# A build-order planner with other costs and a wider urgent class, in an adaLN, Mamba and expert-mixture kernel

## The chip, the cores and the metric

The kernel runs on one core of a Trainium2 chip. A core has five engines, each with its own queue of instructions, which it works off strictly in order: TensorE (PE, matrix products and transposes), VectorE (DVE), ScalarE (ACT), GpSimd (POOL) and SyncE (SP, which here only issues transfers). An instruction whose inputs are not ready holds up everything behind it in its queue. The metric is the device time of one launch in microseconds. Times given as a median are of several unprofiled runs; durations of single instructions come from one profiled execution.

## What is computed

The input x has 4 sequences of 1024 tokens and 512 channels, all in float32. Cut to what matters:

```
mod = silu(c) @ wmod                        # six shifts, scales and gates per sequence
h = layernorm(x) * (1 + ca) + sa
u = causal depthwise convolution of h, 4 taps
dt, B, C = split(u @ xproj.T)               # 128 + 16 + 16
delta = softplus(dt @ dtproj.T + bias)
for every channel d and state n (16 of them), along the 1024 tokens:
    s[t] = exp(delta[t] * A[d, n]) * s[t-1] + delta[t] * B[t, n] * u[t]
y[t] = sum over n of s[t] * C[t, n]  +  u[t] * D_skip
x = x + ga * y
h = layernorm(x) * (1 + cb) + sb
logits = tanh(h @ Wg1.T) @ Wg2.T            # 8 experts, the best 2 per token, softmax of those two
out = sum over the two of score * (silu(h @ Wup[e].T + bup[e]) @ Wdown[e].T + bdown[e])
x = x + gb * out
```

## The kernel before

**Blocks and stages.** The tokens are cut into nine blocks (`BLOCKS`): two of 512 for each of the first three sequences, and 512, 384 and 128 for the last. They are numbered 0 to 8. Each block goes through four stages:

- `front(blk)`: layernorm, convolution, projection, delta. It ends with delta, delta times u (turned) and B in SBUF, and with C's 16 rows written to a scratch array in DRAM.
- The recurrence. It is cut into units, one for each block, channel group of 128 and state, 64 per block and 576 in all, numbered u. A unit is worked on by seven generators: `loads_c` (SP reads one row of C, spread over 128 partitions, tile `cq`, one for two units), `products_b` (ScalarE or GpSimd, tile `dB`), `decays` (ScalarE, the exponential, tile `h`), `inputs` (TensorE turns `dB` into PSUM, tile `pb`), `recurrences` (VectorE, a scan along the tokens), `products_c` (GpSimd, h times C, tile `hc`), `sums` (TensorE adds the `hc` of 16 states into PSUM, tile `acc`). The rings between them are short: 2 `pb`, 3 `hc`, and 4 each of `dB`, `cq` and `h`, of which the last three hold two units.
- `back(blk)` for blocks 0 to 7: VectorE adds the result to x (`residual`), layernorm, transposes (`second_norm`, `turned`), the router with its top two (`router`), each token's place in its expert's rows, and the scatter of the rows to DRAM by GpSimd's indirect transfers (tile `xs`). Beside it `spread` adds the biases and stores the sum (`x1d`).
- The experts. Blocks (0, 1), (2, 3), 4, 5, 6 and 7 form six groups, `GROUPS`, numbered 0 to 5. `tiles(g)` has SP load, for each tile of 128 rows, the rows and 1025 KB of one expert's weights (tile `w`, four buffers, a fifth after the last front), `expert` multiplies (tiles `px`, `pe`, `po`) and stores, and `combine` gathers each token's two rows (tile `xc`, GpSimd) and writes the output. Block 8 takes no tiles: `dense` runs all 8 experts over its 128 tokens (tiles `we`, `pue`, `poe`).

**What sets the order.** All of these are generators that yield a step (engine, cost, what must be there) before they issue its instructions. A planner, the class `Order`, runs while the kernel is built: it keeps a clock for each engine, reckons when each waiting step could begin, takes the engine that can begin first at time t0, and among the steps of that engine that could begin shortly after t0 picks the one with the earliest due time. The instructions are then laid down in that order, for good. The reckoned length of a step is its cost from formulas such as `t_scan` and `t_act`; if it is over 0.03 us, it is multiplied by `PACE` and `WAIT` is added (10% for TensorE, 0.06 us for VectorE, ScalarE and GpSimd). `HANDOFF` is added before another engine may use the result. Where a step can run on one of two engines (`products_b`, `either`, `both`), the planner also picks the engine by these numbers.

"Shortly" is 0.15 us (`TOGETHER`) for an ordinary step. A step whose due time is below `URGENT` (-1000) may begin up to 0.8 us later (`AHEAD`) and is still laid down first. `LAST` makes steps urgent: it is -20000 for the last two blocks, and is added to the due times of the residual, of the way through `back` with its router, of the transposes in `turned` and of the scatters. Tiles and combines have due times from a table, `TILES_DUE`, and do not use `LAST`.

The lines of the profile that matter: 950 scan, 967 product with C, 935 input transposes, 1006 sums, 868 load of C's row, 1040 residual, 1118 and 1253 two steps of the router that wait for other engines, 1335 scatter, 1380 and 1382 loads of a tile's rows and weights, 1448 second product of an expert, 1497 gather of a combine.

Of the kernel before, what the change touches and what calls it, by code (L numbers as in the profile page):

```python
# [30 lines left out]
NBLK = len(BLOCKS)  # L31
# [66 lines left out]

PE, DVE, ACT, POOL, SP = range(5)
HANDOFF = (0.30, 0.17, 0.22, 0.12, 0.0)  # L100
PACE = (1.1, 1.0, 1.0, 1.0, 1.0)
WAIT = (0.0, 0.06, 0.06, 0.06, 0.0)
TOGETHER = 0.15
URGENT = -1e3
AHEAD = 0.8
# [78 lines left out]
class Order:  # L184
# [34 lines left out]
    def run(self):  # L219
        while self.threads:  # L220
            can = [(b, th) for th in self.threads if (b := self.begins(th)) is not None]
            if not can:
                raise RuntimeError("no thread can go on: " + str([th[0].__name__ for th in self.threads]))
            t0, eng, _ = min(can, key=lambda c: c[0][0])[0]
            (t, _, cost), th = min(
                (
                    c
                    for c in can
                    if c[0][1] == eng and c[0][0] <= t0 + (AHEAD if c[1][3] < URGENT else TOGETHER)
                ),  # L230
                key=lambda c: c[1][3],
            )
            self.eng, kb = eng, th[1][4]
            if cost > 0.03:
                cost = cost * PACE[eng] + WAIT[eng]
            self.start = t
            self.free[eng] = t + cost
            self.fin = t + cost + HANDOFF[eng]
            if kb:
                self.moved[eng] = max(self.moved[eng], t + cost) + kb / KB_PER_US  # L240
                self.fin = max(self.moved[eng], t + cost + kb / KB_ALONE) + TRANSFER
            th[2] = self.fin
            th[3] += th[4]
            self.advance(th)
# [28 lines left out]
    return DUE[k] + (f - k) * 150.0 if k >= NBLK else DUE[k] + (f - k) * (DUE[k + 1] - DUE[k])  # L273


LAST = [-2e4 if blk >= NBLK - 2 else 0.0 for blk in range(NBLK)]


@with_exitstack
def adaln_mamba_moe_kernel(  # L280
# [32 lines left out]
    def event(*key):  # L313
        if key not in ev:
            ev[key] = Event()
        return ev[key]
# [542 lines left out]
    def due(u):  # L859
        return DUE[u // PER] + (u % PER + 1) * (DUE[u // PER + 1] - DUE[u // PER]) / PER  # L860
# [120 lines left out]
    def sums():  # L981

        for u in range(N_U):
# [31 lines left out]
            if n == NS - 1:  # L1015
                event("acc", blk, dc).t = o.fin
                o.spawn(residual(blk, dc), due(u) + LAST[blk])

# [17 lines left out]
    def residual(blk, dc):  # L1036
        n = BLOCKS[blk][2]
        yield step(DVE, t_dve(n), event("acc", blk, dc), event("xr", blk, dc // 2))
        xs = xr[blk][dc // 2].t[:, : n // P, dc % 2 * P : (dc % 2 + 1) * P]
        nc.vector.tensor_tensor(xs, xs, acc.pop((blk, dc))[:, :n].rearrange("p (t c) -> p t c", c=P), ALU.add)  # L1040
        acc_ring[dc % 2].give(2 * blk + dc // 2, o.fin)
        event("x1", blk, dc).t = o.fin
        x1_left[blk] -= 1
        if x1_left[blk] == 0:
            if blk + 1 < NBLK:
                o.spawn(back(blk), DUE[blk + 1] + LAST[blk], 1.2)
            else:
                o.spawn(dense(blk), DUE[blk + 1] + LAST[blk], 1.0)

# [110 lines left out]
    def second_norm(blk):  # L1160
# [9 lines left out]
        def turn(dc):  # L1170
            yield from turned(xn, n, dc, b, 3, 4, h2T.t[:, dc, :n], f"b{blk}")
            h2_in[dc].t = o.fin

        for dc in range(DC):
            o.spawn(turn(dc), DUE[blk + 1] + 8.0 + 2.0 * dc + LAST[blk], 2.0)
        return h2T, h2_in

    def back(blk):
# [136 lines left out]
        def scatter(t):  # L1315
            yield step(PE, t_tr(DC), banks, ring("t512B", 4).many(2), combined[g - N_XS])
            h2 = [t512("B", f"h2_{blk}_{t}_{k}") for k in range(2)]
            ph, tag = new_bank(f"ph_{blk}_{t}")
            for dc in range(DC):
                nc.tensor.transpose(ph[:, dc * P : (dc + 1) * P], h2T[:, dc, t * P : (t + 1) * P], ident)  # L1320
            turned_in = Event()
            turned_in.t = o.fin
            yield step(ACT, t_act(512))
            nc.scalar.copy(h2[0].t[:, :D], ph)
            copied = Event()
            copied.t = o.fin
            yield step(DVE, t_dve(512) + 0.15, after=[turned_in])
            nc.vector.tensor_copy(h2[1].t[:, :D], ph)
            for k in range(2):
                nc.vector.tensor_copy(h2[k].t[:, D:], sv[:, k, t : t + 1])  # L1330
            banks.give(tag, o.fin)
            for k in range(2):
                yield step(POOL, 1.2, copied, kb=256)
                nc.gpsimd.tensor_copy(idx[:, k, t : t + 1], to[:, k, t : t + 1])  # L1334
                i = nc.gpsimd.indirect_dma_start(  # L1335
                    out=xs_d[g],
                    out_offset=bass.IndirectOffsetOnAxis(ap=idx[:, k, t : t + 1], axis=0),
                    in_=h2[k].t,
                    in_offset=None,
                )  # L1340
                apart(f"token{g}", i)
                h2[k].done()
            left[0] -= 1
            if left[0] == 0:
                hb.done()
                scattered[g][0] -= 1
                if scattered[g][0] == 0:
                    event("rows", g).t = o.fin

        for t in range(nt):  # L1350
            o.spawn(scatter(t), DUE[blk + 1] + 28.0 + 3.0 * t + LAST[blk], 2.0)

# [378 lines left out]
```

## Time and profile before

| | |
|---|---|
| median of 3 runs | 1471.55 us (1467.81 to 1481.65) |
| the profiled execution | 1473.26 us, span 1471.5 us |
| granted TensorE clock, mean | 0.925 |
| start of the scans of blocks 0 to 8 | 67.7, 191.2, 331.3, 485.3, 646.6, 812.8, 979.1, 1144.1, 1285.7 us |
| last scan | 1387.6 us |
| last expert tile's second product | 1430.3 us |
| bytes moved | 321.65 MB, 219 GB/s over the span |

In the profile a name such as `hc<-h,cq` is a tile and what it is made from, a number such as L967 a line of the kernel, and "x576" a count. A row of waits names who waited, for whom, the sum in us, how often and the longest. A row of stretches gives the length, then for each engine the busy time and the count of its instructions, then TensorE's granted clock, the share of time in which the transfer engines were busy, and GB/s.

### The profile page before, as it was taken

To read this page: it belongs to the slowest core of one execution; us is meant where nothing else is said; L and a number is where in the kernel's file an instruction comes from. 1 tells how busy PE (TensorE), PEld (TensorE's weight loads), DVE (VectorE), ACT (ScalarE), POOL (GpSimd) and SP (SyncE) were. 2 spreads that over 40 slices of the span, in tenths; PEclk is the share of its full clock that TensorE was granted. 3 is DMA by queue.
4 is the path that set the end of the run, shared out by engine and by line. 5 is a ranking of instruction groups with operands and counts; after the bars stand their busy time and mean duration, and the time that the engine had idled before them with its cause. 6 is when DMAs were issued, how large, how long until landed. Compare 5 with 4: busy or idle time off the path is not lost. (4 is left out here: it accounts for less than half of the span.)

```text
span 1471.5 us, 24433 instructions
## 1 busy us (share of the span) xinstructions
PE 1236.6 (84%) x7716; PEld 931.7 (63%) x7716; DVE 1146.8 (78%) x1860; ACT 1041.7 (71%) x2086; POOL 1052.8 (72%) x1239
## 2 busy tenths in 40 slices
PE   5588777878788988988888888998798898888886
PEld 1447564656477766775667766786587776764653
DVE  3569999889887898998887888897879879556343
ACT  3679898689687684899676776888678877455210
POOL 1368897898687676888888656798788878656222
PEclk8699899889799998999699999999999999998798
DMA  4367664758688997654679968688999986986997
GB/s 175 101 161 157 136 160 101 197 127 199 140 243 283 292 273 202 213 159 101 197 257 313 309 210 204 219 269 246 262 252 271 281 221 219 337 249 200 298 311 200
DMA packets 141935, 321.65 MB, mean 219 GB/s; under 512 B 14899, under 2 KB 43475, under 8 KB 128998
## 3 DMA queue, kind: packets, MB, share of 16 engines
q1 hardware_dynamic: 111344, 254.35, 57.9%
q0 software_dynamic: 13888, 32.58, 9.9%
q10 hardware_dynamic: 16566, 33.08, 8.8%
q8 instruction: 63, 1.03, 0.3%
q14 instruction: 74, 0.61, 0.1%
HBM read 245.95 MB, written 82.40 MB: 223 GB/s over the span
## 5 line engine op out<-in xcount | busy, mean ns | idle before, releaser
L967 POOL TENSOR_TENSOR hc<-h,cq 128x512 f32<-128x512 f32 (+2 forms) x576 | 689.5, 1255 | 190.1 <-PE acc L1006 53.4
L920 ACT ACTIVATE h<-delta,a_neg 128x512 f32<-128x512 f32 (+2 forms) x576 | 370.8, 667 | 88.8 <-POOL state L975 44.9
L892 ACT ACTIVATE dB<-duT,bT 128x256 f32<-128x256 f32 x801 | 359.9, 499 | 77.2 <-PE pb L935 74.8
L935 PE MATMUL pb<-ident,dB 128*128 128x128 f32 x2048 | 344.6, 291 | 80.4 <-DVE h L950 64.3
L1006 PE MATMUL acc<-ident,hc 128*128 128x128 f32 x2048 | 340.9, 291 | 75.1 <-POOL hc L967 73.2
L950 DVE TENSOR_TENSOR_SCAN h<-h,state,pb 128x512 f32<-128x512 f32 (+2 forms) x320 | 330.6, 1054 | 50.9 <-PE pb L935 25.8
L935 PEld LDWEIGHTS pb<-ident,dB 128*128 128x128 f32 x2048 | 251.2, 149 | 169.3 <-DVE h L950 85.9
L1006 PEld LDWEIGHTS acc<-ident,hc 128*128 128x128 f32 x2048 | 250.5, 148 | 155.9 <-POOL hc L967 122.3
L950 DVE TENSOR_TENSOR_SCAN h<-h,pb 128x512 f32<-128x512 f32 x256 | 304.4, 1207 | 45.9 <-PE pb L935 37.2
L1420 PE MATMUL pe<-xT,w 128*128 128x128 f32 x1376 | 188.0, 282 | 6.5 <-ACT xT L351 4.8
L1420 PEld LDWEIGHTS pe<-xT,w 128*128 128x128 f32 x1376 | 174.1, 197 | 27.4 <-issue 14.2
L1448 PE MATMUL po<-w,hid 128*128 128x512 f32 x344 | 180.8, 612 | 6.6 <-DVE hid L1440 6.5
L899 POOL TENSOR_TENSOR dB<-duT,bT 128x512 f32<-128x512 f32 (+1 forms) x115 | 119.6, 1061 | 18.4 <-PE pb L935 12.4
L1497 POOL DMA_INDIRECT xc<-xs,idx x56 | 90.4, 1614 | 51.7 <-DMA xc<-xs,idx 29.8
L1458 DVE SCALAR_TENSOR_TENSOR xs<-po,xs,gbh 128x512 f32<-128x512 f32 x86 | 63.6, 740 | 39.7 <-PE po L1448 38.1
L1335 POOL DMA_INDIRECT xs<-h,idx x62 | 64.0, 1032 | 41.3 <-POOL idx L1334 9.2
L1448 PEld LDWEIGHTS po<-w,hid 128*128 128x128 f32 x344 | 54.1, 195 | 24.0 <-issue 11.3
L1438 ACT ACTIVATE th<-pe 128x256 f32<-128x256 f32 x86 | 32.2, 377 | 49.4 <-DVE pe L1431 49.2
L351 ACT COPY xT<-px 128x512 f32<-128x512 f32 x79 | 45.5, 577 | 25.0 <-PE px L1407 24.5
L975 POOL COPY state<-h 128x2 f32<-128x2 f32 x160 | 54.6, 341 | 0.1
L720 PE MATMUL pxd<-xpg,u 128*128 128x160 f32 x256 | 46.2, 329 | 9.4 <-issue 5.6
L1407 PE MATMUL px<-ident,xs 128*128 128x128 f32 x344 | 53.8, 284 | 0.3 <-DVE u L688 0.3
(196 smaller groups left out, 1533.5 us busy)
## 6 DMA issues: line engine op xcount, KB each, us to landing
w<-w_all SPq DMA_DIRECT2D x86, 1025.0 KB, 8.5
cq<-scr SPq DMA_DIRECT2D x224, 256.0 KB, 5.3
xs<-xs SPq DMA_DIRECT2D x86, 256.5 KB, 5.3
xs<-xs SPq DMA_DIRECT2D x86, 256.0 KB, 8.0
xs<-xc ACTq DMA_DIRECT2D x16, 1026.0 KB, 11.7
we<-w_all SPq DMA_DIRECT2D x8, 1025.0 KB, 12.3
xf<-in_x SPq DMA_DIRECT2D x32, 256.0 KB, 6.9
xr<-in_x SPq DMA_DIRECT2D x14, 512.0 KB, 8.9
```

Source lines behind the costliest of these rows:

```text
L892: nc.scalar.activation(dB[u // 2].t[:, t, :], duT_sb[blk][half].t[:, t, :], AF.Identity, scale=bT_sb[blk].t[:, t, n : n + 1],)
L899: engine().tensor_tensor(dB[u // 2].t[:, t0:t1, :], duT_sb[blk][half].t[:, t0:t1, :], bT_sb[blk].t[:, t0:t1, n].unsqueeze(2).to_broadcast( ...
L920: nc.scalar.activation(hs[u // 2].t[:, i, :ln], delta_sb[blk][half].t[:, i, :ln], AF.Exp, scale=a_neg[:, dc, n : n + 1])
L935: nc.tensor.transpose(pbs[u][:, t * P : (t + 1) * P], dB[u // 2].t[:, t, i * P : (i + 1) * P], ident)
L950: nc.vector.tensor_tensor_scan(h, h, pbs.pop(u)[:, :ln], 0.0 if t0 == 0 else state[:, n, dc : dc + 1], ALU.mult, ALU.add,)
L967: nc.gpsimd.tensor_tensor(hcs[u].t[:, :ln], hs[u // 2].t[:, i, :ln], cq[u // 2].t[:, :ln], ALU.mult)
L1006: nc.tensor.matmul(acc[blk, dc][:, t * P : (t + 1) * P], lhsT=src.t[:, t * P : (t + 1) * P], rhs=ident, is_transpose=True, start=False, st ...
L1335: i = nc.gpsimd.indirect_dma_start(out=xs_d[g], out_offset=bass.IndirectOffsetOnAxis(ap=idx[:, k, t : t + 1], axis=0), in_=h2[k].t, in_off ...
L1420: nc.tensor.matmul(pu[:, hc * P : (hc + 1) * P], lhsT=up[:, kc, hc * P : (hc + 1) * P], rhs=xT.t[:, kc, :], start=(kc == 0), stop=(kc == D ...
L1448: nc.tensor.matmul(po, lhsT=hid.t[:, hc * P : (hc + 1) * P], rhs=w.t[:, W_DN + hc * D : W_DN + (hc + 1) * D], start=(hc == 0), stop=(hc == ...
L1458: nc.vector.scalar_tensor_tensor(xs.t[:, :D], po, xs.t[:, D:], gbh[b].t, ALU.mult, ALU.mult)
L1497: nc.gpsimd.indirect_dma_start(out=a, out_offset=None, in_=xs_d[g], in_offset=bass.IndirectOffsetOnAxis(ap=idx_sb[blk][:, choice, t : t + ...
```

## The change

Two things. The planner's two corrections of a step's cost, `PACE` and `WAIT`, go, so that TensorE is reckoned at its full clock and the other engines without the 0.06 us. And `LAST` covers the last four blocks (5, 6, 7 and 8) in place of the last two (7 and 8). No operation, no buffer and no transfer is added or removed; the instructions are laid down in another order, and some steps fall to another engine. All later line numbers shrink by 4.

```
-PACE = (1.1, 1.0, 1.0, 1.0, 1.0)
-WAIT = (0.0, 0.06, 0.06, 0.06, 0.0)
...
             self.eng, kb = eng, th[1][4]
-            if cost > 0.03:
-                cost = cost * PACE[eng] + WAIT[eng]
             self.start = t
             self.free[eng] = t + cost
             self.fin = t + cost + HANDOFF[eng]
...
-LAST = [-2e4 if blk >= NBLK - 2 else 0.0 for blk in range(NBLK)]
+LAST = [-2e4 if blk >= NBLK - 4 else 0.0 for blk in range(NBLK)]
```

## The prediction

> **What bounds the kernel now.** I read the page's busy shares first, then its chain, then a table of stretches, one for each block of the recurrence (cut where the scans at multiples of 64 units start), because the shares are an average over unlike stages.
>
> ```profile
> PE 1236.6 (84%) x7716; PEld 931.7 (63%) x7716; DVE 1146.8 (78%) x1860; ACT 1041.7 (71%) x2086; POOL 1052.8 (72%) x1239
> ...
> PE 7%; DMA 5%; DVE 3%; issue 3%; POOL 2%; ACT 1%; SPq 0%; POOLq 0%; DVEq 0%; ACTq 0%
> ```
>
> Four engines are 71 to 84% busy, and the chain gives no engine more than 7%: no single engine sets the time. What sets it is how well five in-order queues fit together, and that is the thing the change redraws.
>
> ```profile
> core 0: us, PE busy (x) PEld busy (x) DVE busy (x) ACT busy (x) POOL busy (x), PEclk, DMA share, GB/s
> ...
> 812.80:979.10 166.30, 151.94 (x1014) 118.62 (x1013) 143.99 (x222) 126.10 (x245) 120.49 (x121) 0.97 0.79 235
> 979.10:1144.10 165.00, 147.27 (x979) 116.41 (x979) 135.25 (x215) 129.65 (x266) 136.09 (x156) 0.96 0.94 261
> 1144.10:1285.70 141.60, 126.93 (x828) 96.82 (x826) 110.54 (x211) 101.21 (x231) 106.14 (x149) 0.98 0.88 265
> 1285.70:1338.90 53.20, 47.16 (x275) 33.19 (x274) 34.23 (x106) 27.95 (x70) 31.88 (x61) 0.94 0.79 225
> 1338.90:1387.60 48.70, 40.52 (x171) 26.50 (x170) 21.04 (x53) 19.16 (x50) 20.77 (x38) 0.72 0.90 278
> 1387.60:1430.00 42.40, 35.59 (x205) 24.45 (x204) 16.98 (x46) 8.98 (x23) 11.09 (x18) 1.00 1.00 304
> ```
>
> Blocks 5, 6 and 7 take 166, 165 and 142 us, TensorE about nine tenths busy. From 1286 us to the end at 1471.5 (185 us) block 8 and the tail run; block 8's own scans are short (64 of 467 ns, 30 us). The last 10 expert tiles and 8 dense experts each load 1025 KB, and at 1388 to 1430 the DMA share is 1.00. The tail therefore starts when the last router's rows are stored and is then paced by loads.
>
> **The change, part by part.** No arithmetic and no transfer is added. What moves is read by comparing the two built programs' instruction order, engine by engine; positions are in units of the recurrence (one scan each, 0 to 575).
>
> *Reckoned costs.* The change deletes the 10% on TensorE and the 0.06 us on the other three. For 512 columns the old reckoning of a scan was 1.25 us, the new 1.19, the trace has 1.207 and 1.267; the product on GpSimd 1.34, 1.28 and 1.366; ScalarE's 256 columns 0.46, 0.40 and 0.499. On these three the new numbers are the worse ones. For TensorE the row is the granted clock, 0.925 over the run, and 0.96 to 0.98 in blocks 5 to 7. The Trainium skill (TensorE: Matmul & The Clock Gate, What's actually happening) says the clock is either half or full, and full once the array has been busy for one activity window; by that a TensorE nine tenths busy needs no surcharge, and this part costs nothing. By the run's mean 1/0.925 = 1.08, so the plan has TensorE early by 8% of 147 us, 12 us a block where the clock is as in the mean. None of this is time by itself: it counts only where a queue's order gets worse. Up to unit 384 the orders differ by a few units at most (the expert tiles stand within 6 units of where they stood), and the engines' sums barely move: 19 more ScalarE products of 499 ns (+9.5 us) against 7 fewer GpSimd ones of 1061 ns (-7.4 us), 8 delta sums from VectorE to GpSimd, 8 normalizations from ScalarE to VectorE, all on engines under 80%. I take 0 for it, between -6 and +6 us.
>
> *Blocks 5 and 6 urgent.* Before, 18 scans pass between block 5's last residual (385) and its first scatter (403); now 8 (393). For block 6, 454 to 476 becomes 451 to 466. VectorE's router, before cut into five or more pieces with scans between, now stands in two runs of 25 and 24 instructions (23 and 27 for block 6), and every scan behind waits while the router waits for ScalarE, GpSimd and TensorE. The trace has that very pattern for block 7, which is urgent already; here are VectorE's waits in the 31 us behind its residual, then the same 31 us behind the residuals of blocks 7, 5 and 6 in the table's form:
>
> ```profile
> DVE gt L1118 <- ACT pr L1113: 3.2, 1, 3.2
> DVE h L950 <- ACT h L920: 3.1, 1, 3.1
> DVE num L1253 <- PE pp L1226: 2.6, 1, 2.6
> ```
>
> ```profile
> 1290.40:1321.40 31.00, 27.09 (x153) 18.83 (x152) 17.37 (x60) 15.90 (x39) 16.90 (x30) 0.89 0.90 263
> ```
>
> ```profile
> 981.30:1012.30 31.00, 27.56 (x166) 19.73 (x165) 23.10 (x39) 24.32 (x49) 25.55 (x30) 0.94 0.94 259
> ```
>
> ```profile
> 1150.40:1181.40 31.00, 27.19 (x191) 21.34 (x190) 24.45 (x48) 28.04 (x61) 26.75 (x35) 1.00 0.97 291
> ```
>
> VectorE works 17.4 us of 31 in the urgent case, 23.1 and 24.5 in the ordinary ones: 6.4 us less. Twice that is 12.8 us, the upper end. The lower end is 0, since VectorE idles 22 to 31 us in each of these blocks and may catch up. I take 9, nearer the row, because TensorE and GpSimd have little room in which to catch up. What does the urgency buy? Block 5's rows are ready earlier, but its tiles (due by a table) stand where they stood: first at 434 before, 437 now. Block 6's tiles move from 508-541 to 500-526. By count that is one tile more before unit 512 and one fewer after, worth 0 between two stages that are both full.
>
> *Coefficient loads behind weight loads.* SP issues in order, and a weight load waits there until the buffer of the fourth or fifth tile before it is free; every load of C's rows (cq) behind it waits too. Counting for each cq the unit at which the last buffer ahead of it comes free: before, the lead is under 2 units only at 522, 570 and 572. Now it is 1 to -2 at 402 and 410 (block 6), 502, 504 and 510 (block 7), 512, 516, 518 and 520, and 572, 574.
>
> ```profile
> w<-w_all SPq DMA_DIRECT2D x86, 1025.0 KB, 8.5
> cq<-scr SPq DMA_DIRECT2D x224, 256.0 KB, 5.3
> ```
>
> With lead 0, the row lands some 7 us after TensorE reaches that unit (a microsecond to free the buffer, two issues, 5.3 us), while GpSimd normally needs it two units later, 5 us at 2.58 us a unit: 2 to 3 us late. By the Trainium skill (DMA: Bandwidth & Descriptors, Latency and other measured facts) about 2 us of fixed cost would do, and the loads would be in time, cost 0; this trace has no such landing for a 256 KB row, so I go by 5.3. Seven more late loads than before (the clusters count once or twice) by 2.5 us are 17 us, the upper end; GpSimd's lag is buffered by four pairs of h, so the lower end is 0. I take 6: TensorE's new order has the sums trail the inputs by 7 units at 392-424 instead of 3.5, so the buffer is mostly used up there.
>
> *Gathers in block 8.* GpSimd's gathers for block 6's outputs stood as two pairs at 558 and 560, each second waiting for the first's landing:
>
> ```profile
> 1356.28 9.01 DMA xc<-xs,idx
> ```
>
> ```profile
> POOL xc L1497 <- DMA xc<-xs,idx: 5.4, 1, 5.4
> ```
>
> They now stand at 544, 550 and 558, 558. The wait of 5.4 us goes, with a little of what queues behind it: -6, and it passes on to the tail, because the first of the last tiles stands behind these units. The gather at 544 now follows block 6's last tile at 537; between those scans lie 9.3 us in the trace, and its store lands in 8.0, so 0 to +3 is added. I take 0. SP's cq order after 556 and the last scatter (behind 541) are as before, so the tail starts from the same unit.
>
> Sum against the profiled execution's 1473.3 us (span 1471.5): 0 + 9 + 6 - 6 = +9, so 1482. The median of the three runs is 1.7 us lower and their spread is 1467.8 to 1481.7, so I leave 1482 as the median forecast.
>
> **The rivals.** *Faster* (0.12): block 8's stage loosens. Units 512 to 556 take 65 us of which VectorE works 42. With block 6's tiles done by 537 instead of 547 the last loads could start up to 12 us sooner; with the gathers' 6 and nothing lost in blocks 6 and 7 that is 1473 - 18 = 1455. Against it: cq at 512-520 has lead 0 to -2 just there. It decides if that stretch falls under 55 us. *Hidden* (0.14): the costs vanish in idle time, the gathers' gain stays: 1467. *Late rows in full* (0.22): 12.8 + 17 + 6 - 6 = +30, so 1503. *Nothing moves as said*: block 5's tiles indeed don't; that is in my sum. *The sum* (0.52): 1474 to 1494.
>
> **How the numbers follow.** A measurement of this kernel can tell about 1%, here 14.7 us: under 1456.8 is faster, over 1486.3 slower. Of the sum's 0.52 some 0.24 lies above 1486; with 0.22 of late rows that is 0.46 slower. Faster keeps 0.10 of its 0.12; the rest, 0.44, is within 1%. The range for 8 in 10 goes from 1462, inside the hidden case, to 1505.
>
> **What would show it.** Right: blocks 6 and 7 longer by 3 to 12 us each, VectorE waiting at lines L1114 and L1249 (new numbering) in both, GpSimd or its loads of cq late near units 402-410 and 502-520, no 5 us wait of a gather in block 8. Wrong: blocks 6 and 7 as long as before (then the buffers hide all), or the first six blocks differ by over 6 us (then the reckoned costs matter by themselves), or units 512 to 556 well under 65 us.

## The result

The changed kernel takes 1463.55 us (median of 20 runs, 1451.89 to 1472.48) against 1472.15 us before (20 runs beside them, 1465.45 to 1481.65): a ratio of 0.9944, 95% interval 0.9923 to 0.9965. It is 0.6% faster, within 1% of before. The forecast was 1482 us, a loss of 0.7%; the range held the time, the direction was wrong.

The page of the changed kernel, its busy shares and its chain:

```profile
PE 1231.8 (84%) x7716; PEld 929.7 (64%) x7716; DVE 1145.7 (78%) x1861; ACT 1045.8 (72%) x2095; POOL 1045.1 (71%) x1241
...
PE 8%; DMA 2%; DVE 1%; POOL 1%; ACT 1%; issue 1%; SPq 0%; DVEq 0%; POOLq 0%; ACTq 0%
```

The work is the same to within 8 us on every engine, and the span went from 1471.5 to 1462.3 us, so the gain is mostly in waits. The shares of a chain are of the whole span, but the profile could follow this chain back only to 1268.7 us, and that of the kernel before only to 1153.4 us. Of the 14 points here TensorE has 8, and of the 21 before it has 7; of the stages ahead the chain says nothing. The table by stretches of the changed kernel, divided like the one of before (block 6, block 7, then from the first scan of block 8):

```profile
975.10:1138.30 163.20, 146.95 (x982) 115.14 (x982) 139.11 (x220) 130.27 (x268) 133.85 (x154) 0.97 0.91 267
1138.30:1275.20 136.90, 126.42 (x843) 96.39 (x842) 109.75 (x212) 96.76 (x217) 109.22 (x160) 1.00 0.90 281
1275.20:1328.40 53.20, 46.87 (x250) 30.00 (x249) 32.12 (x93) 24.25 (x60) 26.66 (x51) 0.90 0.65 184
1328.40:1382.70 54.30, 42.87 (x191) 26.70 (x189) 26.05 (x65) 23.68 (x62) 28.47 (x53) 0.72 0.90 271
1382.70:1421.50 38.80, 32.08 (x185) 22.17 (x184) 15.63 (x43) 8.04 (x20) 11.19 (x18) 1.00 1.03 306
```

Block 8 starts 10.6 us earlier: 4.0 us of that was there before block 6, 1.8 came in block 6 and 4.7 in block 7, which lasts 136.9 us in place of 141.6 and holds 15 matrix instructions more (843 against 828). Block 8 and the tail after it together are as long as before, 187 against 186 us. TensorE's waits inside block 7 show the difference, first before, then changed:

```profile
PE pb L935 <- DVE h L950: 7.8, 9, 2.6
PE acc L1006 <- POOL hc L967: 5.4, 8, 1.5
```

```profile
PE acc L1002 <- POOL hc L963: 3.3, 4, 1.9
PE pb L931 <- DVE h L946: 1.9, 5, 0.7
```

TensorE waits 5.9 us less for scans there. In the kernel before, 6.3 of the 7.8 us lie in a hole of 22 us in which TensorE works on no expert tile:

```profile
1237.90:1259.90 22.00, 15.38 (x91) 12.28 (x90) 20.91 (x25) 16.00 (x39) 16.97 (x22) 0.84 0.87 298
PE pb L935 <- DVE h L950: 6.3, 7, 2.6
```

In the changed kernel block 6's tiles begin at unit 500 in place of 508, and the longest such hole in block 7 is 6.2 us.

One caution for all that follows. One profile is one execution, and executions of one kernel on one chip lie up to 1.5% apart; a second profile of the kernel before had a span of 1477.4 us and was 5.6 us later at the start of block 6. The 4 us of the first six blocks are no evidence by themselves.

### The profile page after: what moved, and what is told of

It reads as the page before. It is cut to its first block, busy times and chain, and to the rows that moved or that the text cites. A ratio compares the mean times of both kernels' runs of the same rounds, so it can differ in the third digit from the quotient of the medians.

```text
span 1462.3 us, 24472 instructions
## 1 busy us (share of the span) xinstructions
PE 1231.8 (84%) x7716; PEld 929.7 (64%) x7716; DVE 1145.7 (78%) x1861; ACT 1045.8 (72%) x2095; POOL 1045.1 (71%) x1241
## 3 DMA queue, kind: packets, MB, share of 16 engines
q0 software_dynamic: 13888, 32.58, 10.4%
## 5 line engine op out<-in xcount | busy, mean ns | idle before, releaser
L888 ACT ACTIVATE dB<-duT,bT 128x256 f32<-128x256 f32 x820 | 368.1, 499 | 85.3 <-PE pb L931 79.9
L931 PE MATMUL pb<-ident,dB 128*128 128x128 f32 x2048 | 348.1, 293 | 82.5 <-DVE h L946 66.9
L1416 PE MATMUL pe<-xT,w 128*128 128x128 f32 x1376 | 183.9, 278 | 3.4 <-ACT xT L347 3.4
L1416 PEld LDWEIGHTS pe<-xT,w 128*128 128x128 f32 x1376 | 170.2, 193 | 25.8 <-issue 13.3
L895 POOL TENSOR_TENSOR dB<-duT,bT 128x512 f32<-128x512 f32 (+1 forms) x108 | 109.4, 1044 | 30.5 <-PE pb L931 24.6
L1427 DVE TENSOR_TENSOR pe<-pe,w 128x256 f32<-128x256 f32 x86 | 36.1, 420 | 22.9 <-PE pe L1416 19.3
```

Source lines behind the costliest of these rows:

```text
L888: nc.scalar.activation(dB[u // 2].t[:, t, :], duT_sb[blk][half].t[:, t, :], AF.Identity, scale=bT_sb[blk].t[:, t, n : n + 1],)
L895: engine().tensor_tensor(dB[u // 2].t[:, t0:t1, :], duT_sb[blk][half].t[:, t0:t1, :], bT_sb[blk].t[:, t0:t1, n].unsqueeze(2).to_broadcast( ...
L931: nc.tensor.transpose(pbs[u][:, t * P : (t + 1) * P], dB[u // 2].t[:, t, i * P : (i + 1) * P], ident)
L1416: nc.tensor.matmul(pu[:, hc * P : (hc + 1) * P], lhsT=up[:, kc, hc * P : (hc + 1) * P], rhs=xT.t[:, kc, :], start=(kc == 0), stop=(kc == D ...
```

## The experiments

Each group ran on one chip, with the kernel before beside it. Its median there was 1488.65, 1465.47, 1465.25, 1465.12 and 1466.19 us in the five groups. Ratios are against it.

### The two halves of the change, each alone

```
 # c1_last4: the kernel before and
-LAST = [-2e4 if blk >= NBLK - 2 else 0.0 for blk in range(NBLK)]
+LAST = [-2e4 if blk >= NBLK - 4 else 0.0 for blk in range(NBLK)]
```

> The kernel before with only the second half of the change: blocks 5 and 6 urgent too, the reckoned costs left as they were (with the 10% and the 0.06 us). Theory U (the gain comes from the urgency: block 6's tiles fill the hole in front of block 8): this alone gives the whole gain, about -8 us against before, with TensorE's first tile of block 6 near unit 494 in place of 508. Theory R (the gain comes from the other reckoning of costs): within 3 us of before. Theory B (both are needed): between -3 and +5 us. My prediction's own steps would have it at +9 us.

```
 # c1_nopace: the kernel before without PACE and WAIT
-            if cost > 0.03:
-                cost = cost * PACE[eng] + WAIT[eng]
```

> The kernel before with only the first half of the change: costs reckoned without the 10% and the 0.06 us, urgent as before for blocks 7 and 8 alone. Theory U: no gain, 0 to +8 us, since block 6's scatters come later (units 480 to 494 in place of 476 to 487) and its first tile at 514 in place of 508. Theory R: the whole gain, about -8 us, and blocks 0 to 5 shorter by 3 to 5 us in sum. Theory B: 0 to +5 us.

Beside them both kernels of the case once more, unchanged:

> The changed kernel once more, for a second profile and a time on the same chip: -6 to -11 us against before. Where a stage's difference is the change's own it comes back: block 7 (from the scan of unit 448 to that of 512) about 137 us against 142, no wait of over 5 us of a gather in block 8, VectorE busy about 26 of the 31 us behind the residuals of blocks 5 and 6. Where it is chance, above all the -4 us up to block 5, it does not.

> The kernel before once more, for a second profile: time within 3 us of before. Shows how far the start of each block's scans differs between two executions of one program; if by as much as 4 us up to block 6, the -4 us there in the changed kernel's profile says nothing.

| | median, us | ratio, 95% interval |
|---|---|---|
| urgency alone (c1_last4) | 1488.59 | 1.0007 (0.9985 to 1.0030) |
| reckoning alone (c1_nopace) | 1484.80 | 0.9961 (0.9945 to 0.9977) |
| both (c1_after_again) | 1474.87 | 0.9893 (0.9866 to 0.9920) |
| neither (c1_before_again) | 1489.34 | 1.0012 (0.9994 to 1.0031) |

The urgency alone gives nothing, the reckoning alone 4 to 6 us, both together 14 to 16. The halves don't add up: on top of the new reckoning the urgency is worth 10 us. Theory U falls, theory R is too small, and theory B is nearest, though it had expected no gain from the reckoning. Block 7 came back at 136.9 us in the second profile of the changed kernel, against 142.5 in the second of the kernel before. With the urgency alone the hole shrinks too, from 21.0 us in the second profile of before to 9.9, and TensorE waits 2.3 us for scans in block 7 in place of 6.8. Yet block 7 is no shorter (142.2 against 142.5 us), and the tail from the last scan on takes 94.3 us against 88.3: filling the hole is not enough. Up to block 6 the changed kernel's second profile was 2.8 us ahead of that of before.

### One correction at a time, and half of both

```
 # c2_pe_full
-PACE = (1.1, 1.0, 1.0, 1.0, 1.0)
+PACE = (1.0, 1.0, 1.0, 1.0, 1.0)
 # c2_no_wait
-WAIT = (0.0, 0.06, 0.06, 0.06, 0.0)
+WAIT = (0.0, 0.0, 0.0, 0.0, 0.0)
 # c2_half
+PACE = (1.05, 1.0, 1.0, 1.0, 1.0)
+WAIT = (0.0, 0.03, 0.03, 0.03, 0.0)
```

> Of the reckoned costs only TensorE's 10% is gone; the 0.06 us stays and blocks 7 and 8 alone are urgent. Theory P (the planner's cost for TensorE matters, because its own clock is near full while it works): the whole of the -6 us that both reckonings together gave, within 2 us. Theory W (the 0.06 us matters): within 3 us of before. Theory L (any change of the reckoning deals the order anew, and the result is luck): anything from -8 to +12 us, not tied to the size of the step.

> Only the 0.06 us is gone; the 10% on TensorE stays and blocks 7 and 8 alone are urgent. Theory P: within 3 us of before, or slower, since TensorE is now reckoned still longer against the others. Theory W: the whole -6 us, within 2 us. Theory L: anything from -8 to +12 us.

> Both corrections halved (5% and 0.03 us), blocks 7 and 8 alone urgent. Theories P and W: about -3 us, between before and the version with neither (-6 us). Theory L: outside of -6 to 0 as often as inside.

| | median, us | ratio, 95% interval |
|---|---|---|
| without TensorE's 10% | 1478.82 | 1.0076 (1.0049 to 1.0104) |
| without the 0.06 us | 1471.08 | 1.0040 (1.0016 to 1.0063) |
| both halved | 1464.28 | 0.9979 (0.9957 to 1.0002) |

Taking away either correction makes the kernel slower, by 11 and 6 us; halving both changes little. Theories P and W fall. What was left was that the proportions between the engines matter (theory S), or luck (theory L).

### All costs scaled together

```
 # c3_scaled
-PACE = (1.1, 1.0, 1.0, 1.0, 1.0)
-WAIT = (0.0, 0.06, 0.06, 0.06, 0.0)
+PACE = (1.012, 0.92, 0.92, 0.92, 1.0)
+WAIT = (0.0, 0.055, 0.055, 0.055, 0.0)
```

> The kernel before with every reckoned cost multiplied by 0.92, so that the engines keep their proportions (10% and 0.06 us included) and only the handoffs weigh more. Theory S (taking away one correction upsets the proportions, +11 and +6 us; taking both keeps them and makes the handoffs weigh more, which is good for -6 us): about -6 us, within 3. Theory L (luck of the deal): anything from -8 to +12 us.

1465.46 us, ratio 1.0013 (0.9988 to 1.0039): nothing. The part of theory S that should have given the gain, handoffs weighing more, is not seen. Block 7 took 129.4 us in this run's profile, less than in any other, and from block 8's first scan to the end it took 193.7 us in place of 185.8: a short stage alone does not make a fast kernel.

### Which block's urgency

```
 # c2_after_l3: the changed kernel, blocks 6, 7 and 8 urgent
+LAST = [-2e4 if blk >= NBLK - 3 else 0.0 for blk in range(NBLK)]
 # c3_after_b5: the changed kernel, blocks 5, 7 and 8 urgent
+LAST = [-2e4 if blk >= NBLK - 4 and blk != NBLK - 3 else 0.0 for blk in range(NBLK)]
```

> The changed kernel with blocks 6, 7 and 8 urgent, block 5 not. If only block 6's urgency pays (its tiles run out of work in front of block 8) this is as fast as the changed kernel, -8 to -16 us against before, since block 5's tiles stand where they stood. If block 5's matters too, it stays at about -6 us, what the reckoning alone gave. My prediction's step has it 4 to 5 us faster than the changed kernel, for one urgent way less.

> The changed kernel with blocks 5, 7 and 8 urgent, block 6 not; block 6's scatters at 476 to 489, its first tile at 511 in place of 500. If block 6's urgency is what pays beside the reckoning: -6 us against before, what the reckoning alone gave, and block 7 lasts 142 us or more. If block 5's pays: -8 us or more. My prediction's step: 4 to 5 us faster than the changed kernel.

1458.71 us, 0.9937 (0.9906 to 0.9968), with block 6 urgent; 1462.10 us, 0.9972 (0.9943 to 1.0000), with block 5. As good as the changed kernel, and perhaps half of its gain. Without block 6's urgency the profile has a hole of 26.8 us in block 7 and 8.0 us of waits for scans; block 7 lasted 137.7 us there and not the 142 or more that were expected. The intervals overlap and the two ran on different chips, so no block is singled out; that block 5's urgency costs 4 to 5 us is not seen: without it the ratio is 0.9937, with it 0.9944 and 0.9954 on two other chips. Neither is a version that clearly beats the changed kernel.

### The gathers in block 8

```
 # c3_before_gath: the kernel before, in combine()
+            held_back = [event("hc", 575)] if g == 4 and choice == 1 else []
-            yield step(POOL, 1.6, x1_in, event("stored", g), kb=256)
+            yield step(POOL, 1.6, x1_in, event("stored", g), *held_back, kb=256)
 # c3_after_gath: the changed kernel, the same line with
+            held_back = [event("hc", 557 + 2 * choice)] if g == 4 else []
```

> The kernel before, with each token tile's second gather of block 6 held back behind the last product of the recurrence; in the built order only these two gathers move, from unit 560 to 576. My prediction's gather step (the wait of 5.4 us for the first gathers' landing passes on to the end): -6 us. Rival (the wait is slack, because GpSimd is waiting there for rows of C or for TensorE's sums anyhow): within 2 us.

> The changed kernel with block 6's gathers put back to where they stand before (558, 558, 560, 560 in place of 544, 550, 558, 558), all else in the order of the changed kernel. Gather step right: it loses 6 us against the changed kernel, so -2 to -5 us against before; rival: no loss, -8 us or more against before.

Without the wait the kernel before takes 1462.05 us, 0.9987 (0.9954 to 1.0020); with the wait put back the changed kernel takes 1459.31 us, 0.9955 (0.9926 to 0.9984), the same as without (0.9944 and 0.9954 on other chips); 4.0 us of waiting for a gather came back in its profile. So the wait looks slack. The intervals are wide, though: a gain of 6 us lies just inside the first. GpSimd's waits between 1330 and 1390 us, first in the kernel before, then with the second gathers held back:

```profile
POOL hc L967 <- PE acc L1006: 17.4, 9, 10.0
POOL xc L1497 <- DMA xc<-xs,idx: 5.4, 1, 5.4
...
POOL hc L967 <- DMA cq<-scr: 1.0, 1, 1.0
```

```profile
POOL hc L967 <- PE acc L1006: 15.4, 6, 8.1
POOL hc L967 <- DMA cq<-scr: 10.2, 4, 4.4
```

The 5.4 us are gone, and 9.2 us more of waiting for C's rows stand in this one profile.

### Is the gain the change's, or this order's?

The first two of these runs set the halves side by side on one chip. The four after them deal the order anew with a change that has no reason to help or to harm.

> Only the two corrections gone, blocks 7 and 8 urgent, on the same chip as the changed kernel. The first time it gave -6 us (0.9961). Theory R (the other reckoning is the cause): equal to the changed kernel's -8 us within 3. Theory B (both halves are needed): 3 to 8 us behind it.

> The changed kernel beside the one with its first half alone: -8 us against before (0.9944 on one chip, 0.9893 on another).

```
 # c4_before_jitter, c4_after_jitter, c5_nopace_jitter, c5_after_jitter_again
-TOGETHER = 0.15
+TOGETHER = 0.16
```

> The kernel before with the planner's window for ordinary steps at 0.16 us in place of 0.15: a change without any reason for a gain or a loss, which still deals the order anew (some 3000 lines of difference on TensorE). Theory L (orders of one quality scatter by some us; the reckoned costs gain by luck): differs from before by 4 us or more, either way. Theory R or B: within 3 us of before, since the reckoning is the same.

> The changed kernel with the window at 0.16 us in place of 0.15. Theory L: the gain may be gone or doubled, anything from -16 to +4 us against before. Theory R or B: still -6 to -12 us against before, since both halves of the change are there.

And the pair with and without the urgency of blocks 5 and 6, both with the window of 0.16 us and the new reckoning, again on one chip:

> Both corrections gone, blocks 7 and 8 alone urgent, and the window for ordinary steps at 0.16 us: the pair of the next kernel without the urgency of blocks 5 and 6. Theory U2 (under the new reckoning the urgency itself is worth some 10 us, as it was on two chips): 8 us or more slower than the next kernel, so about +15 us against before. Theory L (the 10 us belong to one pair of orders): within 5 us of the next kernel, or faster.

> The changed kernel with the window at 0.16 us once more, beside its pair: about +6 us against before, as the first time (1.0045).

| window | new reckoning, blocks 7 and 8 urgent | new reckoning, 5 to 8 urgent | urgency's worth |
|---|---|---|---|
| 0.15 us, first chip | 1484.80 (0.9961) | 1474.87 (0.9893) | -9.9 us |
| 0.15 us, fourth group | 1469.63 (1.0026, 1.0005 to 1.0047) | 1459.29 (0.9954, 0.9928 to 0.9979) | -10.3 us |
| 0.16 us, fifth group | 1464.82 (0.9991, 0.9962 to 1.0019) | 1470.36 (1.0037, 1.0011 to 1.0064) | +5.5 us |

With the window at 0.16 us the changed kernel is slower than before, in both groups (1.0045, 1.0019 to 1.0071, in the fourth), and the urgency's gain turns into a loss of 5.5 us. The kernel before moved only to 1.0020 (0.9993 to 1.0046), less than the 4 us that theory L had expected of it. So the 10 us are real for the pair of orders at 0.15 us, on two chips, but the urgency as such does not have that worth: it gave 0 with the old reckoning, -10 with the new one, and +5.5 with the new one and the other window. The reckoning alone was -4 us on one chip and +4 on another. Of the theories L fits best, with one new deal for each kernel behind it; its forecasts were wide, so it risked little.

What the 10 us are made of can be read in the pair of the fourth group. Block 7 by stretches and TensorE's largest wait in it, first without the urgency, then with it:

```profile
1126.80:1272.00 145.20, 125.99 (x772) 95.31 (x770) 114.10 (x207) 102.72 (x235) 99.84 (x142) 0.91 0.77 241
```

```profile
PE pb L931 <- DVE h L946: 13.1, 13, 3.0
```

```profile
1129.30:1264.10 134.80, 125.87 (x843) 96.43 (x842) 109.78 (x211) 96.77 (x217) 109.43 (x160) 1.00 0.89 282
```

```profile
PE pb L931 <- DVE h L946: 1.9, 5, 0.7
```

Without the urgency all 12 tiles of block 6 stand behind unit 512 (first at 514); with it six stand ahead (first at 500). TensorE then does 71 matrix instructions more in 10.4 us less: it waits 11 us less for scans, and the granted clock is 1.00 in place of 0.91. The hole without tiles is 34.8 us long without the urgency, 6.2 with it. The profiles of the same two orders on the first chip agree: 145.3 and 136.9 us, 13.7 and 1.9 us of waits for scans, a clock of 0.92 and 1.00. Block 8's stage, with those tiles gone, is 6.6 us shorter too (108.1 against 114.7).

At 0.16 us the order without urgency had less of that hole (23.3 us, first tile at 510; block 7 lasts 137.8 us). The one with urgency had none over 6.6 us, but its block 7 was no shorter (139.8 us), and it paid at the end. Its stretch from the last scan to the end, below that of its pair:

```profile
1386.90:1465.40 78.50, 58.83 (x327) 39.78 (x325) 29.12 (x69) 10.87 (x27) 20.63 (x25) 0.94 0.91 267
```

```profile
1391.40:1474.60 83.20, 63.98 (x347) 43.18 (x345) 30.86 (x72) 11.61 (x29) 20.67 (x25) 0.93 0.92 259
```

It is the second that has the urgency: 4.7 us longer, with 20 matrix instructions more. Its order leaves seven expert tiles behind the last unit, that of its pair six. Over all the profiles the tail tends to grow with this count: five tiles left over, 69.6 to 79.5 us; six, 76.7 to 88.3; seven, 83.1 to 92.8; eight (the urgency alone), 94.3. The ranges overlap, and the changed kernel by itself had 77.7 to 84.4 us. No run changed the hole or the count of tiles left over by itself, so that they make the 10 us and the 5.5 us is read from the traces and not tested.

## Why the prediction was wrong

*What bounds the kernel.* The chain's 7% for TensorE was taken as a share of a chain over the whole span. That chain began at 1153.4 us, so it was 7 of the 21 points that it had, and it told nothing of blocks 5 and 6.

*The reckoned costs, 0 between -6 and +6.* The size was right: -4 and +4 us on two chips. But each correction alone moved the time by +11 and +6, so the bound was not one for a reckoning as such. The argument that the new numbers are worse told nothing: the clock was 1.00 in block 7 with the changed order and 0.91 with another, TensorE being busy for 93% and 87% of the stage, so not even TensorE's own row was fixed, and nine tenths busy did not mean a full clock.

*Blocks 5 and 6 urgent, +9: the step that failed.* On top of the new reckoning the urgency measured -9.9 and -10.3 us (0 with the old reckoning, +5.5 with the other window). The price of +9 came from block 7's router in the kernel before, where VectorE worked 6.4 us less than elsewhere. That row compared unlike scans. Here are the scans alone (L950) in the same three stretches, behind the residuals of blocks 7, 5 and 6:

```profile
1290.40:1321.40 31.00, 5.16 (x12) 0.89 0.90 263
981.30:1012.30 31.00, 12.95 (x11) 0.94 0.94 259
1150.40:1181.40 31.00, 13.02 (x13) 1.00 0.97 291
```

Behind the urgent router as many scans passed as elsewhere. They took 7.8 us less because block 8's scans are of 128 columns, those of blocks 6 and 7 of 512 and 384. VectorE's other work, 12.2 us, was more than in the other two stretches (10.2 and 11.4). So the row showed no cost of urgency. The 31 us behind the residuals of blocks 5 and 6 in the changed kernel, and the wait that should have been 3 us:

```profile
977.20:1008.20 31.00, 27.35 (x170) 19.80 (x169) 25.90 (x54) 22.71 (x46) 24.94 (x33) 0.94 0.91 257
```

```profile
1141.40:1172.40 31.00, 27.19 (x185) 20.59 (x184) 26.31 (x51) 24.64 (x53) 25.32 (x37) 1.00 0.90 271
```

```profile
DVE gt L1114 <- ACT pr L1109: 0.3, 1, 0.3
```

VectorE worked 25.9 and 26.3 us, more than in the ordinary way before (23.1 and 24.5). Behind block 5's residual 8 scans passed in place of 11, so the urgent way did hold scans up there, but block 6 was no longer for it (163.2 us against 165.0). The run of 25 instructions that I counted as one blocked stretch also holds a later block's layernorm and steps of tiles, so VectorE had other work in it. The other half of the step, "worth 0 between two stages that are both full", failed as well. The table said nine tenths busy and I read it as full; of the 14.7 us in which TensorE was not busy in block 7, 7.8 were waits for scans, most of them where no tile was queued. That hole stood in the trace of before (1237.9 to 1259.9 us), and I had named its filling in the count of tiles but gave it no price. Its filling goes with a block 7 that is 4.7 us shorter; what it is worth by itself no run shows, and so the cause of the 10 us stays open in part.

That the measured time lay inside the range owes nothing to this step: the range was wide enough for the hidden case.

*Late rows of C, +6: about 0, read from the trace.* In the changed kernel the row for unit 402 was issued at 1033.4 us and its product began at 1049.4; for 410, 502 to 520, 572 and 574 it was 6 to 19 us. GpSimd's products waited 2.2 us for such rows in the whole run, 12.9 before:

```profile
POOL hc L967 <- DMA cq<-scr: 12.9, 7, 7.3
```

```profile
POOL hc L963 <- DMA cq<-scr: 2.2, 1, 2.2
```

I had set the loads against TensorE's inputs, while most of these products came three to nine units behind them. The lag of 7 that I took for a used-up buffer was the cover.

*The gathers, -6: about 0.* The wait went, as forecast, and no gain was seen (-2 us with an interval of -7 to +3 in one kernel, none in the other). Waits for C's rows and for sums stand beside it in the traces.

*The rivals.* The faster one named block 8's stage and was to decide by units 512 to 556 falling under 55 us; they took 74. The gain came ahead of it. "Hidden" (1467 us) had most of the costs right and came near in time, but by luck: the gathers' gain that it counted on was not seen.

## What to carry to other kernels

Where a planner lays out in-order queues, a constant of its cost model has no price of its own: a different constant deals a different order, and such orders lay between 0.9893 and 1.0076 of the kernel before here. Before a gain of half a per cent is put down to an idea, deal again with a meaningless change (a window 0.01 us wider) and see whether the gain stays. When two stretches are compared by an engine's busy time, compare instructions of one size. And read a stage's missing tenth by what the busiest engine waits for in it and by what work could have stood there, before calling the stage full.

## What the runs showed of the hardware

TensorE's granted clock went with the order: in block 7 it was 0.91 and 0.92 in two profiles of one order, with 13 us of waits for scans, none over 3.0 us, and 1.00 in three profiles of the changed kernel, with 1.9 us of them. The sum of the waits does not fix it: with 10.5 us of them (new reckoning alone, window 0.16 us) it was 0.98. In the record of the run with 0.91 the clock stands only at full or half, and in block 7 there are five pieces at half, of 3.4 or 6.8 us, 27 us together. Four of the five begin right after 3.4 us in which TensorE was busy for 1.0 to 1.9 us. One such pair of stretches:

```profile
1238.58:1241.99 3.41, 1.50 (x10) 1.06 (x10) 3.41 (x3) 1.77 (x5) 3.41 (x6) 1.00 0.92 317
1241.99:1248.82 6.83, 5.27 (x24) 4.97 (x25) 5.92 (x7) 6.31 (x17) 4.11 (x5) 0.50 1.06 355
```

So short waits that fall close together stand ahead of a slower clock in this trace, though no single one is long.

Chips differ as well: the kernel before took 1488.65 us on one and 1465 to 1472 on the others, and the reckoning alone was faster by 0.4% on the slow one and slower by 0.3% on another, both clear of their intervals.
